# A message-passing layer on one core: the value product moved to the front of each step, the ranks to its end, and a bias written by ScalarE

## Chip, cores and metric

The kernel runs on one core of a Trainium2 chip. The metric is the device time of one execution in microseconds (us); the verdict rests on runs without a profile, and the traces come from one profiled execution of each kernel. The engines are TensorE (PE in the profile, PEld for its weight loads), VectorE (DVE), ScalarE (ACT), GpSimd (POOL) and SyncE (SP, which here only issues transfers).

## The reference

The program is one graph layer: 12,500 nodes with 128 features, 412,500 edges sorted by destination, 20 edge features.

```python
def ssp(x):
    return jax.nn.softplus(x) - LOG2
h = jnp.maximum(_layernorm(x), 0.0) @ W_in2f
Wij = (ssp(edge_attr_20 @ W_f1 + b_f1) @ W_f2 + b_f2) * edge_weight[:, None]
x_ij = h[dst] * Wij
agg = jax.ops.segment_sum(x_ij, src, num_segments=12500)
out = x + (ssp(agg @ W_o1 + b_o1) @ W_o2 + b_o2)
```

The gather goes by `dst`, which is sorted, and the sum by `src`, which is not. So each edge's message has to be carried to its source node's place.

## The kernel before

**Tiling.** The edges are cut into 806 chunks of 512 (`CH`), each of four tiles of 128 edges (`QT`). One pass of the main loop is one step: `step(k)` does one stage of work for each of some ten neighbouring chunks, so that each engine finds work. A chunk goes through these parts, each with a letter in the step's order:

- `Z` (L879): the hidden product, edge features by W_f1, into one of two PSUM banks `z`; done for chunk k+4. A sorted chunk (below) takes L875 instead.
- `L` (L885, L492, L493): ScalarE's three passes of softplus for chunk k+3, giving `a`.
- `E` (L892): VectorE joins `z` and `a` to `r` for chunk k+2; this also frees the bank `z`.
- the bias of the value (L1008 on TensorE, a product of ones with the bias; L1012 is the same write by ScalarE, `bias()` chooses by `"parts" in kept`). Letter `A` writes it for chunk k+1, letter `I` for chunk k+2.
- `V` (L1020): the value product, `r` by W_f2, onto the bias in a PSUM bank `v`; chunk k+1.
- `W` (L1000): VectorE builds the selection `at` for chunk k+3, and `P` (L1041): TensorE picks the 128 node rows of h for each edge with it, into another bank `v`; chunk k+2.
- `H` (L1057, L1064): ScalarE scales the picked rows by the edge weight to `hg`; chunk k+1.
- `M` (L1070): VectorE multiplies value and `hg` to the message `o` of chunk k. Then the chunk before it is scattered: four `DMA_INDIRECT` on GpSimd (L1086) write 129-float rows to HBM tables `slots`. `scatter()` makes the first of them wait for `sigs[-1]`, the last signal of TensorE that letter `U` kept (from chunk 24 on).
- `B` (L901), `R` (L950, L922), `T` (L930, L942, L945, L946): one-hot blocks, running ranks in the PSUM bank `counts`, and the reduction to the slot that each message goes to. They run up to six chunks ahead.
- `C` (L1172, L1166) and `S` (L1194): the sums. `slots` rows of finished segments are loaded back (`m`, L1152), VectorE compares them with place numbers (`to`), TensorE adds them up in `sums`; `K` (L1225) adds a block to the result.
- `X` (L1351 to L1404): TensorE's products of a presort of 80 chosen chunks (`SORT`), whose messages are later gathered and not scattered. `presorts()` is advanced once a step after chunk 14, and by `X` when its next piece is one of TensorE's. It ends by chunk 372 (`"idx" in kept`).
- `J`: small column work.

**What sets the order.** There is no scheduler: each engine does its instructions in the order in which the letters call them, and waits only for semaphores. Steps 0 to 7 take `FIRST_ORDER`, all others `ORDER`. Three banks `v` are handed round by the list `v_free`: pick, bias and value of neighbouring chunks take them, `H` and `M` give them back. The message tiles `o` are ten (`BACK`), and the second and third products of `V` and `P` wait for the scatters of ten chunks before (`behind`). Loads on SP wait for `sigs[-1]` as well (`covered`).

After the last chunk, the remaining sums and the output layer follow (some 170 us).

Of the kernel before, what the change touches and what calls it, by code (L numbers as in the profile page):

```python
# [60 lines left out]
def gnn_kernel(  # L61
# [33 lines left out]
    parts = next(n for n in range(3, SUMT + 1) if SUMT % n == 0)  # L95
# [47 lines left out]
    def sbuf(name, shape, dtype=F32):  # L143
        return const.tile(shape, dtype, name=name)
# [50 lines left out]
    idx = sbuf("idx", [P, NBLK], I32)  # L195
# [207 lines left out]
    kept = {}  # L403
# [224 lines left out]
    with tc.tile_pool(name="edge", bufs=2) as edge, tc.tile_pool(  # L628
# [860 lines left out]
        HEAD, SLOW, FREE, RA, RB = 8, 5, 12, 2, 6  # L1489
# [11 lines left out]
        def part(name, upto, make):  # L1501

            for j in range(made.get(name, -1) + 1, min(upto, NCH - 1) + 1):
                make(*of(j))
                made[name] = j
# [37 lines left out]
        def ahead(k):  # L1543
            return k + min(LR, RA + max(k, 0) // RB)

        ORDER, FIRST_ORDER = "TMHPRXEBCKSAVUZWJL", "MTBHVPWENISLJZRU"

        def step(k, units=(), order=None):

# [3 lines left out]
            def message(j):  # L1553
                if j in vs:
                    g, c = of(j)
                    g.message(c, vs[j], hgs.pop(j))
                    v_free.append(vs.pop(j))
                    waiting.append(j)
                    scatter()
# [95 lines left out]
            for c, u in due_gathers.get(k, ()):  # L1655
                c.gather(u)
            parts = {
                "E": lambda: part("end", min(k + EZ, made["log"]), hidden_end),
                "M": lambda: message(k),
                "N": lambda: message(k + 1),  # L1660
                "T": tops_of,
                "X": midway,
                "B": lambda: part("blocks", ahead(k + 1), blocks),
                "C": compares,
                "K": keep,
# [10 lines left out]
                "L": lambda: part("log", min(k + LL, made["hidden"]), hidden_log),  # L1676
                "U": signal,
            }
            for p in order or (FIRST_ORDER if k < HEAD else ORDER):
                parts[p]()  # L1680

        zeros = {}
# [35 lines left out]
        pos, k = 0.0, 0  # L1718
        jobs = {}
        for i, c in enumerate(collects[:-1]):  # L1720
            for u, (_, nb, _, nt) in enumerate(c.units):
                n = nb * nt
                for j in range(n):
                    pos = max(pos, at[i])
                    k = max(k, int(pos) + 1)
# [116 lines left out]
        with tc.manual_schedule():  # L1842
# [48 lines left out]
            hgs[0] = groups[0].picked(0, ps[0])  # L1891
            v_free.append(ps.pop(0))
            step(0, (), "M")
            part("log", 1, hidden_log)
            part("window", 1, window)
# [15 lines left out]
            part("blocks", 2, blocks)  # L1911
            part("window", 2, window)
            step(1, (), "M")
            next(moved, None)
            part("log", 2, hidden_log)
# [4 lines left out]
            for k in range(0, max(NCH, max(units) + 1)):  # L1920
                for seg, d in zeros.get(k, ()):
                    seg.clears.append(nc.sync.dma_start(*d).ins.name)
                now = units.get(k, ())
                for c, u in now:
                    if u == 0:
                        for i in range(AHEAD):
                            c.load(i)
                if k == NCH:
                    kept["rest"] = True
                step(k, now)  # L1930

                for _ in range(STAGES[k] if k < len(STAGES) else 1):
                    for m in h[:1]:
                        if next(m, 1) == 1:
                            h.pop(0)
                if k == 0:
                    early[1] = load_x(1)
                if k in ROWS:
                    kept["rows"] = ROWS[k]
                if k > NEXT - 3:  # L1940
                    next(aside, None)
                if k >= PRE and kept.get("want") != "mid":
                    kept["want"] = next(before_all, "mid")
                if k >= XK:
                    next(x_early, None)
# [136 lines left out]
```

## Time and profile before

| | us |
|---|---|
| median of three runs | 5035.33 (5027.56 to 5047.56) |
| the profiled execution's own time | 5080.24 |
| its span, first to last instruction | 5078.5 |
| steps 8 to 371 (with the presort), from the trace | 66.2 to 2024.3 |
| steps 372 to 805, from the trace | 2024.3 to 4910.9 |

No engine is busy for more than 77% of the span. In a row of the views, "idle before" is how long the engine stood still just ahead of those instructions, and the names behind the arrow are what ended it; "issue" and "remote" are waits whose end the profile cannot put to an instruction. The starts of TensorE's instructions are recorded, the ends of matmuls are modelled.

### The profile page before, as it was taken

The numbers are of one execution on the slowest core, as the hardware profiler recorded it, in microseconds if no ns is written. First come the engines' busy times: TensorE is split into PE (matmuls) and PEld (weight loads), VectorE is DVE, ScalarE is ACT, GpSimd is POOL, SyncE is SP. The second block draws the span as 40 slices with busy tenths as digits, with TensorE's granted clock in tenths as the row PEclk, the third lists the DMA queues.
The fourth block names the chain that finished last, engine by engine and source line by source line (L and its number), as shares of the span: only waits on it lengthen the run. The fifth ranks groups of instructions, "written<-read, shape, count | busy, mean of one in ns | idle before, by whom it ended". The sixth has DMA issues, their size and how long they took to land.

```text
span 5078.5 us, 78295 instructions
## 1 busy us (share of the span) xinstructions
PE 3908.5 (77%) x24114; PEld 2965.9 (58%) x24114; DVE 3200.6 (63%) x7639; ACT 2722.9 (54%) x6941; POOL 2957.1 (58%) x3100
## 2 busy tenths in 40 slices
PE   5667777777777777888888877778878887877879
PEld 3444545544444445666666665666666666666667
DVE  5767767666565667666655655565666666665657
ACT  6666666666666665555544444444444444444423
POOL 5555555555555556555666665666666665555543
PEclk8887878888777878999988988898999999898889
DMA  5566666665545655666655555655556655645547
GB/s 156 161 193 191 193 184 181 185 172 163 142 133 143 177 140 156 202 195 204 217 163 177 166 162 158 204 184 166 172 174 213 198 174 176 207 158 174 160 138 218
DMA packets 586009, 892.45 MB, mean 176 GB/s; under 512 B 164366, under 2 KB 368324, under 8 KB 585582
## 3 DMA queue, kind: packets, MB, share of 16 engines
q1 hardware_dynamic: 483584, 656.09, 43.8%
q0 software_dynamic: 100736, 230.77, 13.7%
q8 instruction: 192, 3.15, 0.3%
q14 instruction: 235, 1.93, 0.1%
q10 hardware_dynamic: 1262, 0.52, 0.0%
HBM read 490.45 MB, written 396.56 MB: 175 GB/s over the span
## 4 chain that ended last, share of the span: by engine, by line


## 5 line engine op out<-in xcount | busy, mean ns | idle before, releaser
L1086 POOL DMA_INDIRECT slots<-o,slot x2903 | 2806.1, 967 | 1819.1 <-issue 1287.3
L885 ACT ACTIVATE a<-z,bf 128x512 f32<-128x512 f32 x806 | 556.5, 690 | 1840.1 <-remote 838.1
L1194 PE MATMUL sums<-to,m 128*128 128x128 f32 x8296 | 1200.0, 299 | 181.1 <-issue 168.9
L1194 PEld LDWEIGHTS sums<-to,m 128*128 128x128 f32 x8296 | 1142.9, 213 | 267.5 <-issue 229.6
L1070 DVE TENSOR_TENSOR o<-v,hg 128x512 f32<-128x512 f32 x806 | 554.5, 688 | 1180.0 <-issue 566.0
L1020 PEld LDWEIGHTS v<-wf,r 128*128 128x128 f32 x6448 | 1002.7, 221 | 440.9 <-issue 383.1
L1020 PE MATMUL v<-wf,r 128*128 128x128 f32 x6448 | 1005.8, 305 | 49.4 <-issue 41.4
L1057 ACT ACTIVATE hg<-v,rcut 128x128 f32<-128x128 f32 x2904 | 818.9, 366 | 152.1 <-remote 83.5
L879 PE MATMUL z<-f,wf1z 128*128 128x512 f32 x1452 | 812.1, 641 | 40.2 <-DVE r L892 19.8
L1172 DVE TENSOR_TENSOR to<-counts,m 128x512 f32<-128x512 bf16 (+3 forms) x824 | 582.7, 740 | 347.9 <-remote 129.5
L1041 PEld LDWEIGHTS <-at 126*128 126x128 bf16 x2896 | 219.2, 103 | 722.1 <-issue 391.8
L892 DVE SCALAR_TENSOR_TENSOR r<-z,nbf,a 128x512 f32<-128x512 f32 x806 | 597.6, 741 | 1.7 <-ACT a L493 0.9
L493 ACT ACTIVATE a<-a,half 128x512 f32<-128x512 f32 x806 | 581.9, 722 | 26.2
L1008 PE MATMUL v<-hb 128*128 128x512 bf16 x784 | 339.8, 433 | 279.7 <-DVE o L1070 218.8
L930 DVE TENSOR_REDUCE top<-counts 128x4 f32<-128x392 f32 x726 | 403.9, 556 | 213.6 <-remote 148.9
L492 ACT ACTIVATE a<-a 128x512 f32<-128x512 f32 x806 | 507.9, 630 | 25.5
L1041 PE MATMUL v<-near,at 126*128 126x128 bf16 x2896 | 308.8, 232 | 257.4 <-DVE at L1000 133.3
L950 PE MATMUL counts<-inb,rest_of 128*128 128x392 f16 x719 | 258.8, 360 | 298.4 <-issue 149.2
L922 PEld LDWEIGHTS <-after 128*128 128x128 f16 x726 | 74.4, 102 | 339.0 <-issue 337.5
L879 PEld LDWEIGHTS z<-f,wf1z 128*128 128x128 f32 x1452 | 244.4, 210 | 47.3 <-issue 24.3
L922 PE MATMUL counts<-inb,after 128*128 128x392 f16 x726 | 264.0, 364 | 8.1 <-issue 7.8
L1000 DVE TENSOR_SCALAR at<-rel,prow 126x512 bf16<-126x512 bf16 x724 | 260.7, 360 | 0.0
(240 smaller groups left out, 2839.5 us busy)
## 6 DMA issues: line engine op xcount, KB each, us to landing
m<-slots SPq DMA_DIRECT2D x430, 258.0 KB
rel<-rel_d SPq DMA_DIRECT2D x201, 504.0 KB
m<-slots SPq DMA_DIRECT2D x178, 322.5 KB
m<-slots SPq DMA_DIRECT2D x139, 387.0 KB
f<-in_f_t SPq DMA_DIRECT2D x100, 512.0 KB
slots<-o,slot POOLq DMA_INDIRECT x2903
slots<-zero SPq DMA_DIRECT2D x88, 387.0 KB
slots<-zero SPq DMA_DIRECT2D x58, 516.0 KB
```

The lines of the kernel that those rows point to most:

```text
L492: nc.scalar.activation(a, a, AF.Exp, scale=-1.0)
L493: nc.scalar.activation(a, a, AF.Ln, bias=half, scale=0.5)
L879: kept["mm"] = nc.tensor.matmul(z_ps[k % 2], wf1z[:, k, :], self.f, start=True, stop=True)
L885: nc.scalar.activation(self.a[k], z_ps[k % 2], AF.Abs, bias=bf1)
L892: nc.vector.scalar_tensor_tensor(self.r[k], z_ps[k % 2], nbf1, self.a.pop(k), op0=ALU.max, op1=ALU.add)
L1020: mm = nc.tensor.matmul(v[:, i, :], r[:, i * P:(i + 1) * P], wf2, start=False, stop=True, skip_group_check=True)
L1041: mm = nc.tensor.matmul(ps[:, i, :], at[:, i * P:(i + 1) * P], near, start=i == 0, stop=i == QT - 1, skip_group_check=True)
L1057: act = nc.scalar.activation(hg[:, i, :], ps[:, i, :], AF.Copy, scale=cut[:, i:i + 1])
L1070: nc.vector.tensor_mul(self.o[c][:, :, :P], v, hg)
L1086: put = nc.gpsimd.indirect_dma_start(out=views[j % VIEWS], out_offset=bass.IndirectOffsetOnAxis(ap=self.slot[:, j:j + 1], axis=0), in_=o[: ...
L1172: nc.vector.tensor_tensor(to[:, :n, :], count_ps[:, None, :].to_broadcast([P, n, P]), m[:, :n, P:].to_broadcast([P, n, P]), op=ALU.is_equal)
L1194: kept["mm"] = nc.tensor.matmul(self.acc[b // QT][:, i, :], m[:, j, :P], to[:, j, :], start=t == 0, stop=t == self.tiles(b) - 1)
```

## The change

From step 8 on the letters stand in another order. Up to step 371 `ORDER` is `EMTBCKHAVXSPIWJZRLU`, from 372 on `LATE_ORDER`, the same without `X`. At step 372 the key `parts` is dropped, so that `bias()` writes with ScalarE (L1012) from there on. `I` now writes the bias two chunks ahead, so `A` finds it done. `U` is still the last letter, and the last product ahead of it is now one of `R` where `V` stood before.

```diff
-        ORDER, FIRST_ORDER = "TMHPRXEBCKSAVUZWJL", "MTBHVPWENISLJZRU"
+        ORDER, FIRST_ORDER = "TMHPRXEBCKSAVUZWJL", "MTBHVPWENISLJZRU"
+        LATE_ORDER, LATER = "EMTBCKHAVSPIWJZRLU", 372
+        ORDER = "EMTBCKHAVXSPIWJZRLU"
...
-            for p in order or (FIRST_ORDER if k < HEAD else ORDER):
+            if k == LATER:
+                assert "idx" in kept
+                del kept["parts"]
+            for p in order or (FIRST_ORDER if k < HEAD else ORDER if k < LATER else LATE_ORDER):
                 parts[p]()
```

By engine, a step's letters read before and after: TensorE `P R X S A V Z` and `V X S P I Z R`; VectorE `T M E B C K W J` and `E M T B C K W J`; ScalarE `H L` and `H L`, from 372 on `H I L`.

TensorE in the second stage, before. `v` with its number is one of the three banks, `hb_76` holds the bias parts; the first row is the last product of a pick:

```order
L1041 MATMUL v_161<-near,at 128x128
L950 LDWEIGHTS rest_of
L950 MATMUL counts<-inb,rest_of 128x392
L922 LDWEIGHTS after
L922 MATMUL counts<-inb,after 128x392
L1194 MATMUL sums_157<-to,m 128x128 x8
L1008 LDWEIGHTS hb_76
L1008 MATMUL v_160<-hb_76 128x512
L1020 MATMUL v_160<-wf_63,r 128x128 x4
L879 MATMUL z_155<-f,wf1z 128x512
```

The same stretch of work after, from the hidden product of one step to the pick of the next:

```order
L879 MATMUL z_155<-f,wf1z 128x512
L950 LDWEIGHTS rest_of
L950 MATMUL counts<-inb,rest_of 128x392
L922 LDWEIGHTS after
L922 MATMUL counts<-inb,after 128x392
L1020 MATMUL v_159<-wf_63,r 128x128 x4
L1194 MATMUL sums_158<-to,m 128x128 x8
L1041 LDWEIGHTS at
L1041 MATMUL v_159<-near,at 128x128
```

The bias product is gone from TensorE, the value product stands ahead of the sums, the pick behind them, and the ranks behind the hidden product. Before, every value product goes to bank `v_160`; after, the banks take turns, and a value product's bank comes back in the pick behind the sums.

VectorE in the second stage, before: one step, from `at` to `at`.

```order
L1000 TENSOR_SCALAR at<-rel,prow 126x512
L930 TENSOR_REDUCE top<-counts 128x4
L1070 TENSOR_TENSOR o<-v_160,hg 128x4x128
L892 SCALAR_TENSOR_TENSOR r<-z_156,nbf_67,a 128x512
L901 TENSOR_TENSOR inb<-of_block,blk_30709 128x392
L1172 TENSOR_TENSOR to<-counts,m 128x512
L1000 TENSOR_SCALAR at<-rel,prow 126x512
```

And after:

```order
L1000 TENSOR_SCALAR at<-rel,prow 126x512
L892 SCALAR_TENSOR_TENSOR r<-z_156,nbf_67,a 128x512
L1070 TENSOR_TENSOR o<-v_160,hg 128x4x128
L930 TENSOR_REDUCE top<-counts 128x4
L901 TENSOR_TENSOR inb<-of_block,blk_30707 128x392
L1172 TENSOR_TENSOR to<-counts,m 128x512
L1000 TENSOR_SCALAR at<-rel,prow 126x512
```

`r` has moved ahead of the message, and the reduction `top` behind it.

ScalarE in the second stage, before:

```order
L1057 ACTIVATE hg<-v_161,rcut 128x128 x4
L1064 ACTIVATE o<-place 128x4
L885 ACTIVATE a<-z_155,bf_66 128x512
L492 ACTIVATE a<-a 128x512
L493 ACTIVATE a<-a,half 128x512
```

And after:

```order
L1057 ACTIVATE hg<-v_160,rcut 128x128 x4
L1064 ACTIVATE o<-place 128x4
L1012 ACTIVATE v_160<-bf_84 128x512
L885 ACTIVATE a<-z_156,bf_66 128x512
L492 ACTIVATE a<-a 128x512
L493 ACTIVATE a<-a,half 128x512
```

The bias write stands between the scaling and the softplus, into the bank that the scaling has just read.

## The prediction

> **What bounds the kernel now.** I read the page's busy line first, then the two stages (with the presort, and after it), then TensorE's waits in each, then the timeline of one period, and last the rows of the engines that the change loads or unloads.
>
> ```profile
> span 5078.5 us, 78295 instructions
> PE 3908.5 (77%) x24114; PEld 2965.9 (58%) x24114; DVE 3200.6 (63%) x7639; ACT 2722.9 (54%) x6941; POOL 2957.1 (58%) x3100
> ```
>
> No engine is full: the time lies in round trips between engines. By stretch (columns: us, busy time of PE, PEld, DVE, ACT and POOL with counts, granted clock, DMA share, GB/s):
>
> ```profile
> 66.20:2024.30 1958.10, 1407.74 (x7896) 949.95 (x7896) 1296.29 (x3638) 1251.18 (x3290) 1129.01 (x1162) 0.81 0.58 167
> 2024.30:4910.90 2886.60, 2320.85 (x14999) 1866.28 (x14999) 1748.10 (x3674) 1380.40 (x3481) 1736.50 (x1802) 0.91 0.57 180
> ```
>
> The first stage is 364 steps of 5.38 us, the second 434 of 6.65. TensorE is idle for some 550 us in each (1958.1 - 1407.7, 2886.6 - 2320.9). What it waited for, by instruction group, two rows of the first stage and then three of the second (busy, mean ns of one | idle before, what ended it):
>
> ```profile
> L1008 PE MATMUL v<-hb 128*128 128x512 bf16 x351 | 159.8, 455 | 239.9 <-DVE o L1070 191.8 <-issue 29.0 <-DVE top L918 12.8
> L950 PE MATMUL counts<-inb,rest_of 128*128 128x392 f16 x293 | 109.5, 374 | 258.8 <-issue 130.0 <-DVE top L930 119.1 <-DVE pre L1400 6.0
> ...
> L1194 PE MATMUL sums<-to,m 128*128 128x128 f32 x7666 | 1115.3, 299 | 169.3 <-issue 164.8 <-DMA near<-h 1.6
> L1008 PE MATMUL v<-hb 128*128 128x512 bf16 x434 | 180.4, 416 | 39.9 <-DVE o L1070 26.9 <-issue 10.5 <-DVE top L918 2.0
> L1041 PE MATMUL v<-near,at 126*128 126x128 bf16 x1704 | 180.2, 229 | 250.8 <-DVE at L1000 133.3 <-issue 80.3 <-DVE to L1172 12.5
> ```
>
> In the first stage TensorE waits ahead of the bias product for VectorE's message, which gives the bank back, and ahead of the ranks for the reduction `top`. In the second it waits mostly ahead of the pick for `at`. One period of the second stage (start, duration, engine, what, idle before it):
>
> ```profile
> 2403.55 1.05 PE L1020 MATMUL v<-wf,r 128*128 128x128 f32 x8
> 2404.44 1.02 PE L879 MATMUL z<-f,wf1z 128*128 128x512 f32 x2
> ...
> 2405.30 0.39 PE L1041 MATMUL v<-near,at 126*128 126x128 bf16 x4
> ...
> 2405.52 0.33 PE L950 MATMUL counts<-inb,rest_of 128*128 128x392 f16 x1
> ...
> 2405.69 0.33 PE L922 MATMUL counts<-inb,after 128*128 128x392 f16 x1
> ...
> 2406.11 0.96 POOL L1086 DMA_INDIRECT slots<-o,slot  x1 [0.30 <-issue]
> ...
> 2408.98 0.69 ACT L885 ACTIVATE a<-z,bf 128x512 f32<-128x512 f32 x1 [4.56 <-remote]
> 2408.99 0.69 DVE L1070 TENSOR_TENSOR o<-v,hg 128x512 f32<-128x512 f32 x1 [4.41 <-issue]
> ...
> 2409.65 0.95 POOL L1086 DMA_INDIRECT slots<-o,slot  x1 [2.58 <-issue]
> ...
> 2418.53 0.96 POOL L1086 DMA_INDIRECT slots<-o,slot  x1 [0.31 <-issue]
> ...
> 2421.27 0.69 DVE L1070 TENSOR_TENSOR o<-v,hg 128x512 f32<-128x512 f32 x1 [1.70 <-remote]
> ...
> 2421.93 0.96 POOL L1086 DMA_INDIRECT slots<-o,slot  x1 [2.44 <-issue]
> ```
>
> This is the picture to keep. The value product ends at 2404.6 and the hidden product at 2405.5, yet the message and the softplus that need nothing else start only at 2408.98, both at once: TensorE's signals reach the others up to 4.4 us late. They come after GpSimd has run dry (its last scatter ends at 2407.07). Then the message runs, GpSimd gets its next scatters, and after eight of them, two chunks, it is dry again: 2409.65 to 2421.93 is 12.28 us for two steps, of which 8 x 1.26 = 10.1 is scattering and 2.4 to 2.6 the gap. So in the second stage two things set the pace together: round trips that carry a late signal, and GpSimd's two chunks to a period. GpSimd's scatters, the first stage and the second:
>
> ```profile
> L1086 POOL DMA_INDIRECT slots<-o,slot x1162 | 1130.2, 973 | 830.1 <-issue 476.4 <-PE v L1020 96.7 <-ACT o L1064 70.2
> ...
> L1086 POOL DMA_INDIRECT slots<-o,slot x1707 | 1643.1, 963 | 963.0 <-issue 794.4 <-ACT a L885 57.6 <-DVE inb L901 21.9
> ```
>
> Back to back, one takes 0.97 + 0.30 = 1.27 us: 1476 us of the first stage's 1958, 2156 of the second's 2887.
>
> **The change, part by part.** I sum against the profiled execution's 5080.24 us; the median of the runs is 5035.33, a factor of 0.9912, and the sum is scaled by it at the end.
>
> (a) *First stage, the bias and value products.* Before, the value product ends a step, the message waits for its signal, and the next bias product waits for the message. After, the bias goes two chunks ahead into the bank that ScalarE's scaling has freed, and the value product needs only that and `r`. The message's bank is now needed by the pick, behind the next value product, the presort's products and the sums. The signal's slack grows by at least one value product (1.05 us) and mostly by a half step or more. The wait of 239.9 us has 351 products behind it; a typical one:
>
> ```profile
> 861.06 0.69 DVE L1070 TENSOR_TENSOR o<-v,hg 128x512 f32<-128x512 f32 x1 [5.45 <-issue]
> ...
> 861.80 0.58 PE L1008 MATMUL v<-hb 128*128 128x512 bf16 x1 [4.79 <-DVE o L1070]
> ```
>
> Bounds: all of it goes (-240), or all comes back ahead of the ranks or the pick (0). The ranks' loop is not loosened: before, ranks to `top` to ranks; after, ranks to `top`, blocks, compare, ranks, since the compare reads the same PSUM bank that the ranks write. That loop still passes one late signal a step, and its row (258.8 us) is as large as the one that goes. I take half: **-120 us**.
>
> (b) *Second stage, the pick.* Before, `at` stands on VectorE behind a compare that waits for the ranks of the same step, so the pick of the next step waits for a late signal of the ranks. After, the compare follows the ranks of the step before, and `at` of a pick is built a whole step ahead. So the 250.8 us can go; bounds -251 and 0. But here each period also holds GpSimd's two chunks and its gap, which the order of TensorE does not shorten; TensorE's gain turns into waiting unless a third chunk's signal slips into the period. I take a quarter, nearest to that bound: **-60 us**.
>
> (c) *Second stage, the bias on ScalarE.* TensorE loses 434 products. Their issue distance, from a bias product to the value product behind it, is small:
>
> ```profile
> 2414.41 0.38 PE L1008 MATMUL v<-hb 128*128 128x512 bf16 x1
> 2414.41 1.08 PEld L1020 LDWEIGHTS v<-wf,r 128*128 128x128 f32 x8
> 2414.62 1.05 PE L1020 MATMUL v<-wf,r 128*128 128x128 f32 x8
> ```
>
> 434 x 0.21 = 91 us, and the wait ahead of them was 39.9: at most -131. ScalarE gets as many writes; the first steps show what one takes, and the second row is where ScalarE stands idle in the second stage:
>
> ```profile
> L1012 ACT ACTIVATE v<-bf x22: 580/601/602, 13.5 to 142.1; 128x512 f32<-128x512 f32 x22
> ...
> L885 ACT ACTIVATE a<-z,bf 128x512 f32<-128x512 f32 x431 | 296.8, 689 | 1355.7 <-remote 588.6 <-PE z L879 332.5 <-PE counts L922 206.7
> ```
>
> 434 x 0.601 = 261 us, just ahead of a softplus that waits 1355.7 / 431 = 3.1 us each time. Behind the write is queued that softplus, then `r`, then (new) the message, which now stands behind `r` on VectorE. While the 3.1 us of cover last, the write costs nothing; without them it would be up to +261. I take **0** for both ends together.
>
> (d) *The signal that releases scatters and loads.* It was the value product's, it is now the ranks'. Both are the last of their step but one product, and between two of them lies one step of TensorE's work in either order. From release to the next signal TensorE needed, before, the message (0.69), bias and value products (0.21 + 1.05); after, the message, `top`, blocks and compares, then the ranks:
>
> ```profile
> L1172 DVE TENSOR_TENSOR to<-counts,m 128x512 f32<-128x512 bf16 (+3 forms) x731 | 522.4, 750 | 317.9 <-remote 129.5 <-PE z L879 67.9 <-PE v L1020 48.4
> L1070 DVE TENSOR_TENSOR o<-v,hg 128x512 f32<-128x512 f32 x432 | 297.3, 688 | 757.7 <-issue 416.0 <-remote 198.7 <-PE v L1020 42.3
> L930 DVE TENSOR_REDUCE top<-counts 128x4 f32<-128x392 f32 x423 | 234.9, 555 | 11.4 <-remote 4.9 <-PE z L879 4.3 <-issue 2.0
> L901 DVE TENSOR_TENSOR inb<-of_block,blk 128x392 f16<-128x392 bf16 x421 | 148.7, 353 | 0.0
> ```
>
> That is 0.69 + 0.56 + 0.35 + 1.7 compares x 0.75 + ranks 0.5 = 3.4 us against 2.0. GpSimd has 4 x 1.26 = 5.0 us of work in that time, so I take **0**; the other end is the rival below. A signal that comes sooner could not run GpSimd faster than it does: no gain here.
>
> (e) Everything else moves without a price: `r` ahead of the message waits for a softplus of the step before, covered by the 757.7 us for which VectorE stands idle ahead of the message; the presort's products stand behind the value product (1.05) where they stood behind pick and ranks (0.39 + 0.5), so ScalarE's and VectorE's half of a presort piece has the same time; SP's loads wait for the same signal as the scatters.
>
> Sum: -120 - 60 + 0 + 0 = -180; 5080 - 180 = 4900, times 0.9912 = **4860 us**.
>
> TensorE's products keep program order, says the Trainium skill (TensorE: Matmul & The Clock Gate, "Step-by-step: what each phase is for"): only weight loads are pulled ahead. By that alone a wait that goes would be met again at the next instruction that needs the same signal, (a) would be 0 and the sum 5080 - 60 = 5020, scaled 4976 us. The rows of the first stage are on its side in part: bias product and ranks wait in turn, 239.9 and 258.8.
>
> **The rivals.**
> 1. *No change.* GpSimd's period of two chunks holds, and in the first stage the ranks' wait swallows what the bias product's gave. For it: 12.28 us a period whatever TensorE does in between. Against it: the first stage's GpSimd is dry for 1958 - 1476 = 482 us, so there it is not the bound. Time: 5035, give or take 25. Chance 0.17.
> 2. *Slower: the ranks' signal comes too late for the second chunk of a period.* It decides from 5.0 us after the release: 3.4 us worked out in (d) plus a lateness of 1.6. Signals in the middle of a period were late by more (4.4 above). Each time GpSimd then runs dry after one chunk and pays a gap of 2.5 us more. The second stage has 1707 / 4 = 427 scattered chunks, 213 periods; a third of them gives +178, all +530. The same in the first stage would add to it. Time: about 5210, from 5080 to 5560. Chance 0.23.
> 3. *More: the clock goes up too.* The granted clock is 0.81 in the first stage, where TensorE idles for 28% of it, and 0.91 in the second, where it idles for 20%. If the first stage got the second's clock, its 1407.7 us of busy time would shrink by 1 - 0.81/0.91 = 11%, 155 us, on top: about 4710. Chance 0.10. The Trainium skill's clock gate (TensorE: Matmul & The Clock Gate, Part 1) bears on it: an idle window of about 3.4 us halves the clock, a busy one restores it; the gaps of 4 to 5 us above are of that length, and the new order would have to close them whole.
>
> **How the numbers follow.** My forecast has 0.50. With rival 3, faster has 0.60; rival 1 is same, 0.17; rival 2 slower, 0.23. About 0.5% is what a measurement of this kernel can tell from no change. The range: below, (a) and (b) both at three quarters give -370, scaled 4670, and I go to 4660; rival 3's lower part lies outside. Above, it takes in rival 1 and the mild half of rival 2, to 5130. Outside remain some 0.07 below and 0.13 above. If it is faster, 4700 to 4990 is the likely part.
>
> **What the trace after would show.** (a) right: no wait for the message ahead of a bias product, and the ranks' idle in the first stage not above some 380 us; wrong: L950 or L1041 idles there by 500. (b) right: L1041's wait for `at` below 100 us. (c) right: L1012 at 0.6 us, 434 more, ScalarE's idle ahead of L885 smaller by as much. (d) right: still eight scatters between GpSimd's long gaps in the second stage; wrong: four. What would make the forecast wrong is (d) above all, since late signals are not explained by anything that this trace shows, and I assume that they stay as late as they are.

## The result, and the profile after

The changed kernel takes 5097.89 us (median of 4 runs, 5091.94 to 5109.76) beside 5034.40 for the kernel before: a ratio of 1.012, with a 95% interval of 1.0102 to 1.0138. It is slower by 63 us, where I had forecast 4860 and faster. The runs below were made in five sets: in three, as in all numbers so far, the kernel before takes about 5040 us and TensorE's signals come late, in the other two it takes 3992 us and they come promptly, and each run is compared with the kernel before of its own set.

The page of the changed kernel, its span and busy line:

```profile
span 5097.5 us, 76863 instructions
PE 3795.7 (74%) x23681; PEld 2890.9 (57%) x23681; DVE 3202.9 (63%) x7639; ACT 2952.9 (58%) x7374; POOL 2963.4 (58%) x3100
```

The stages, with the columns as in the prediction (us, busy time of PE, PEld, DVE, ACT, POOL, granted clock, DMA share, GB/s), from the value product of chunk 8 to those of chunks 372 and 805. First the changed kernel, then a second profile of the kernel before, which I took because the first one (5080 us) was 45 us above the median:

```profile
68.90:2079.10 2010.20, 1361.21 (x7873) 924.04 (x7872) 1286.29 (x3630) 1253.32 (x3286) 1128.10 (x1159) 0.82 0.56 162
2079.10:4926.80 2847.70, 2253.90 (x14588) 1815.93 (x14586) 1762.17 (x3685) 1606.93 (x3912) 1740.96 (x1802) 0.90 0.58 183
```

```profile
59.70:2010.80 1951.10, 1401.54 (x7897) 950.15 (x7897) 1296.24 (x3638) 1252.73 (x3291) 1130.32 (x1163) 0.81 0.58 168
2010.80:4856.70 2845.90, 2310.85 (x15000) 1843.66 (x14999) 1748.37 (x3676) 1378.62 (x3480) 1735.95 (x1801) 0.91 0.58 183
```

So the loss lies in the first stage: 2010.2 against 1951.1, +59 us (+52 against the first profile). The second stage is unchanged: 2847.7 against 2845.9. The 2886.6 us of the first profile, on which my sum stood, were a long execution. The granted clock hardly moved (0.82 and 0.90 against 0.81 and 0.91).

What TensorE waited for in the first stage, after (busy, mean ns of one | idle before, what ended it):

```profile
L1008 PE MATMUL v<-hb 128*128 128x512 bf16 x350 | 152.6, 436 | 71.6 <-issue 47.2 <-ACT hg L1057 24.0
L1041 PE MATMUL v<-near,at 126*128 126x128 bf16 x1164 | 127.1, 239 | 180.2 <-DVE o L1070 98.9 <-issue 67.7 <-DVE r L892 13.4
L950 PE MATMUL counts<-inb,rest_of 128*128 128x392 f16 x293 | 113.2, 386 | 96.5 <-DVE top L930 53.5 <-issue 39.4 <-DVE to L1172 3.6
L1351 PE MATMUL sums<-pick,pre 107*128 107x2 bf16 x320 | 21.2, 170 | 188.7 <-ACT pre L1407 124.5 <-issue 62.5 <-ACT hb L454 1.7
L1373 PE MATMUL sums<-ones,pre 128*98 128x1 f16 x320 | 35.3, 214 | 75.4 <-DVE pre L1344 68.8 <-issue 4.2 <-DVE pre_d L1333 2.4
```

In the second profile of before the same rows read:

```profile
L1008 PE MATMUL v<-hb 128*128 128x512 bf16 x351 | 160.7, 458 | 285.7 <-DVE o L1070 237.7 <-issue 31.0 <-DVE top L918 9.8
L950 PE MATMUL counts<-inb,rest_of 128*128 128x392 f16 x293 | 109.1, 372 | 220.7 <-issue 107.3 <-DVE top L930 106.9 <-DVE pre L1400 4.7
L1041 PE MATMUL v<-near,at 126*128 126x128 bf16 x1164 | 124.6, 234 | 3.1 <-issue 1.5 <-DVE at L1000 1.4 <-DVE early_room L266 0.2
L1373 PE MATMUL sums<-ones,pre 128*98 128x1 f16 x320 | 31.8, 203 | 0.0
L1351 PE MATMUL sums<-pick,pre 107*128 107x2 bf16 x320 | 21.3, 170 | 9.8 <-ACT pre L1407 4.9 <-issue 4.8
```

The wait for the message ahead of the bias product is gone, and the ranks' wait fell from 220.7 us to 96.5. Part of the message's wait is met again at the pick, L1041, which now stands idle for 180.2 us, 98.9 of them for the message, where it had 3.1. And two rows that were hardly there have grown: products of the presort, L1351 and L1373, now wait 264 us where they had waited 10.

In the second stage, after:

```profile
L1041 PE MATMUL v<-near,at 126*128 126x128 bf16 x1704 | 186.6, 230 | 65.3 <-issue 42.6 <-DVE o L1070 10.2 <-DMA slots<-o,slot 5.8
L950 PE MATMUL counts<-inb,rest_of 128*128 128x392 f16 x418 | 148.4, 355 | 236.4 <-DVE to L1172 133.3 <-issue 69.2 <-DVE to L1166 31.9
```

The pick's wait for `at` (133.3 us in the first profile, 97.3 in the second) is gone, and the ranks wait for the compare instead (133.3 and 31.9 us): no less waiting, one instruction further on. That the figure 133.3 stands twice is chance.

GpSimd's scatters in the first stage, of the second profile of before and of the changed kernel:

```profile
L1086 POOL DMA_INDIRECT slots<-o,slot x1163 | 1131.7, 973 | 821.1 <-issue 468.8 <-PE v L1020 123.3 <-ACT o L1064 63.0
```

```profile
L1086 POOL DMA_INDIRECT slots<-o,slot x1159 | 1129.4, 974 | 883.1 <-issue 331.8 <-ACT a L885 174.4 <-ACT a L492 133.7
```

GpSimd's idle time grew by 62 us, as the stage did. Where it grew can be read from the scatters' single rows in the trace: a presorted chunk has no scatter, so GpSimd always runs dry there. From chunk 25 to 371 the 73 gaps behind such chunks add up to 281 us in the second profile of before and 391 after, all other gaps of over 0.5 us to 218 and 156. Of the 73, before, 14 are over 5 us; after, 40, most of them 7 to 8. One of these, from the timeline of the changed kernel (start, duration, engine, line, what, idle before it):

```profile
860.09 1.03 PE L1404 MATMUL sums<-pre,pre_d 128*107 128x512 bf16 x4
...
867.75 0.96 POOL L1086 DMA_INDIRECT slots<-o,slot  x1 [0.30 <-issue]
868.98 0.60 ACT L1407 ACTIVATE pre<-sums 107x512 bf16<-107x512 f32 x1 [4.37 <-remote]
...
869.63 0.25 PE L1351 MATMUL sums<-pick,pre 107*128 107x2 bf16 x4 [2.98 <-issue]
870.47 0.57 DVE L1344 TENSOR_TENSOR pre<-counts,pre 128x392 f16<-128x392 bf16 x1 [5.43 <-remote]
...
871.09 0.49 PE L1373 MATMUL sums<-ones,pre 128*98 128x1 f16 x4 [1.21 <-DVE pre L1344]
...
875.18 0.53 PE L922 MATMUL counts<-inb,after 128*128 128x392 f16 x1
...
876.47 0.96 POOL L1086 DMA_INDIRECT slots<-o,slot  x1 [7.76 <-ACT a L885]
```

The presort's product ends at 861.1, but ScalarE's copy of it starts only at 868.98, 0.3 us after GpSimd's last scatter: the late signal. ScalarE had been idle for 4.37 us by then. TensorE, which has issued its next value product, stands at L1351 for that copy. Only then can it do the pick, the hidden product and the ranks, and GpSimd's next scatter waits for the ranks' signal; it starts 0.76 us after their end. In 39 of the 40 long gaps TensorE's longest stop is at L1351 or L1373, and the scatter starts 0.75 us (median) after the ranks.

### The profile page after: what moved, and what is told of

Same layout as the page of the kernel before. It is cut to its first block, busy times and chain, and to the rows that moved or that the text cites. A ratio compares the mean times of both kernels' runs of the same rounds, so it can differ in the third digit from the quotient of the medians.

```text
span 5097.5 us, 76863 instructions
## 1 busy us (share of the span) xinstructions
PE 3795.7 (74%) x23681; PEld 2890.9 (57%) x23681; DVE 3202.9 (63%) x7639; ACT 2952.9 (58%) x7374; POOL 2963.4 (58%) x3100
## 4 chain that ended last, share of the span: by engine, by line
## 5 line engine op out<-in xcount | busy, mean ns | idle before, releaser
L1194 PEld LDWEIGHTS sums<-to,m 128*128 128x128 f32 x8296 | 1097.8, 208 | 272.9 <-issue 264.1
L1020 PEld LDWEIGHTS v<-wf,r 128*128 128x128 f32 x6448 | 953.9, 214 | 179.3 <-issue 134.8
L1020 PE MATMUL v<-wf,r 128*128 128x128 f32 x6448 | 980.5, 298 | 68.0 <-issue 63.4
L879 PE MATMUL z<-f,wf1z 128*128 128x512 f32 x1452 | 881.0, 691 | 33.9 <-issue 18.5
L1041 PE MATMUL v<-near,at 126*128 126x128 bf16 x2896 | 316.7, 234 | 245.5 <-issue 110.2
L1041 PEld LDWEIGHTS <-at 126*128 126x128 bf16 x2896 | 245.3, 105 | 318.7 <-issue 249.8
L879 PEld LDWEIGHTS z<-f,wf1z 128*128 128x128 f32 x1452 | 277.0, 216 | 82.0 <-issue 53.4
L1012 ACT ACTIVATE v<-bf 128x512 f32<-128x512 f32 x455 | 273.7, 602 | 0.0
```

The lines of the kernel that those rows point to most:

```text
L879: kept["mm"] = nc.tensor.matmul(z_ps[k % 2], wf1z[:, k, :], self.f, start=True, stop=True)
L1020: mm = nc.tensor.matmul(v[:, i, :], r[:, i * P:(i + 1) * P], wf2, start=False, stop=True, skip_group_check=True)
L1041: mm = nc.tensor.matmul(ps[:, i, :], at[:, i * P:(i + 1) * P], near, start=i == 0, stop=i == QT - 1, skip_group_check=True)
L1194: kept["mm"] = nc.tensor.matmul(self.acc[b // QT][:, i, :], m[:, j, :P], to[:, j, :], start=t == 0, stop=t == self.tiles(b) - 1)
```

## The experiments

The stage times are those of each run's own profile. The last column counts the gaps of over 5 us behind presorted chunks. The ratio is to the kernel before in the same set.

| kernel (sets with late signals) | median us | ratio, interval | stage 1 | stage 2 | long gaps |
|---|---|---|---|---|---|
| before, second profile | 5026 (one run) | | 1951 | 2846 | 14 |
| after, again | 5076.87 | 1.007, 1.0032 to 1.0107 | 2022 | 2851 | 43 |
| bias_on_tensor_2 | 5087.52 | 1.0097, 1.007 to 1.0124 | 2020 | 2839 | 41 |
| new_second_only_2 | 5042.03 | 0.9985, 0.996 to 1.001 | 1957 | 2846 | 19 |
| signal_behind_value_2 | 4998.19 | 0.9904, 0.9882 to 0.9926 | 1884 | 2877 | 9 |
| first_stage_signal | 4965.02 | 0.9857, 0.9829 to 0.9884 | 1893 | 2836 | 12 |
| message_first | 4965.78 | 0.9848, 0.9811 to 0.9885 | 1884 | 2843 | 8 |
| presort_behind_ranks | 5028.36 | 0.9984, 0.9959 to 1.0009 | 1948 | 2842 | 8 |
| presort_last_signal_early | 5032.29 | 0.9992, 0.9971 to 1.0013 | 1951 | 2843 | 5 |
| message_first_presort_last | 5045.43 | 1.0013, 0.9992 to 1.0034 | 1960 | 2844 | 12 |
| signal_ahead_of_value | 5185.90 | 1.0297, 1.0269 to 1.0325 | 2099 | 2840 | 53 |
| scatters_ahead_loads_behind | 5175.27 | 1.0266, 1.0231 to 1.0302 | 2091 | 2833 | 54 |

| kernel (sets with prompt signals) | median us | ratio, interval | stage 1 | stage 2 |
|---|---|---|---|---|
| new_first_only | 3992.43 | 1.0005, 0.9996 to 1.0014 | 1490 | 2287 |
| new_second_only | 3986.72 | 0.9986, 0.9977 to 0.9996 | 1484 | 2274 |
| signal_behind_value | 3982.11 | 0.9976, 0.9968 to 0.9985 | 1483 | 2269 |
| bias_on_tensor | 3986.39 | 0.9991, 0.9982 to 1.0001 | 1484 | 2270 |
| signal_behind_pick | 3989.00 | 0.9990, 0.9980 to 0.9999 | 1488 | 2273 |
| presort_ahead_of_value | 3989.05 | 0.9991, 0.9981 to 1.0000 | 1487 | 2286 |

**First set: which stage, which part.** The edits, each against the changed kernel:

```diff
 new_first_only:      - LATE_ORDER = "EMTBCKHAVSPIWJZRLU", del kept["parts"]
                      + LATE_ORDER = "TMHPRXEBCKSAVUZWJL", parts kept
 new_second_only:     - ORDER = "EMTBCKHAVXSPIWJZRLU"   + ORDER = "TMHPRXEBCKSAVUZWJL"
 signal_behind_value: + ORDER = "EMTBCKHAVUXSPIWJZRL", LATE_ORDER = "EMTBCKHAVUSPIWJZRL"
 bias_on_tensor:      - del kept["parts"]
```

new_first_only: 

> New order for chunks 8 to 371 alone; from 372 on the order of before, bias on TensorE. Theory A (the loss is in the first stage: after a presorted chunk, whose step has no scatter, GpSimd waits for the ranks at the end of a whole TensorE step, 7 to 9 us instead of 2.5 to 5): slower than before by the first stage's 52 us or more, 5085 to 5140 us. Theory B (the loss is in the second stage, by the bias on ScalarE or the late ranks, and a long profiled run of before hides it): within 25 us of before, 5010 to 5060.

new_second_only: 

> The order of before up to chunk 371; from 372 on the new order with the bias on ScalarE. Theory A: the second stage gains some 40 us, 4980 to 5020 us. Theory B: slower than before by all of the change's loss, 5080 to 5110.

signal_behind_value: 

> The changed kernel, but scatters and loads wait for the value product again (its signal is taken behind V) and not for the ranks. Theory A: the 40 gaps of over 5 us behind presorted chunks shrink from some 7.6 to 4.5 us, about -120 us: 4950 to 5010 us, and no more than 15 such gaps. Rival C (the presort's products behind the value product bring their signals late to ScalarE and VectorE, whatever the scatters wait for): the gaps stay, 5080 to 5115.

bias_on_tensor: 

> The changed kernel with the bias still written by TensorE from chunk 372 on; the order stays. This prices term (c) of the prediction, which was 0 between -131 and +261 us. Theory A: the second stage's time is set by the late signals and GpSimd, and the writer of the bias does not matter: 5098 give or take 25. Theory B: ScalarE's 434 writes of 0.60 us delay the softplus, and the kernel is faster without them by 60 us or more, below 5040.

In these four the signals came promptly, and all lie within 0.24% of before (table). That is a result of its own: without late signals neither half of the change moves the time by more than 0.14%. The whole change was not run there. The order of before in its first stage there (in new_second_only), by stretch and by GpSimd:

```profile
55.80:1539.50 1483.70, 1208.69 (x7898) 831.83 (x7897) 1293.36 (x3639) 1235.90 (x3290) 1115.93 (x1145) 0.94 0.76 220
```

```profile
L1086 POOL DMA_INDIRECT slots<-o,slot x1145 | 1117.3, 976 | 368.1 <-issue 236.1 <-ACT o L1064 13.6 <-DMA slots<-o,slot 11.6
```

1484 us is close to the 1476 us that the scatters take back to back. The 73 gaps behind presorted chunks add up to 39 us here, against 281 with late signals, so there was no loss to explain, and the theories, whose times all rest on late signals, were not told apart.

**Second set, with late signals.** The changed kernel, the kernel before, and two of the edits above once more.

after_again: 

> The changed kernel again. The runs so far fall into two kinds: executions of 5034 to 5098 us, in which TensorE's signals reach the others several us late, and the four of the stage experiments at 3982 to 3992 us, with no such signal. If signals arrive promptly here too, theory A expects no loss, since no gap behind a presorted chunk exists to grow: 3975 to 3995 us beside 3992 for before. If they are late, it expects the loss again: 1.0 to 1.4% above before.

before_again: 

> The kernel before again, for a second profile. With prompt signals: near 3992 us, first stage about 1490 us (GpSimd's 1476 with hardly a gap). With late signals: near 5035 us, and the stage that is shorter than in the profiled run of 5080 us tells where the rest of the change's loss lies.

signal_behind_value_2: 

> The changed kernel, with scatters and loads waiting for the value product. With late signals, theory A: 4950 to 5010 us and no more than 15 gaps over 5 us behind presorted chunks in the first stage; rival C (the presort's products behind the value product are what comes late): 5080 to 5115 and some 40 gaps. With prompt signals: within 0.5% of before, as in its first run (3982).

new_second_only_2: 

> New order and ScalarE's bias from chunk 372 on alone. With late signals, theory A: the second stage gains some 40 us of 5034, so 4980 to 5020; theory B (the loss is in the second stage): 5080 to 5110. With prompt signals: within 0.5% of before, as in its first run (3987).

The loss is there again, and again in the first stage (2022), but with 0.7% it is smaller than the 1.0 to 1.4% expected. The profiled execution of after_again is the longest of its four (5111 against a median of 5077), so its 2022 is at the upper end. The new order from 372 on alone costs and gains nothing (5042, stage 2846): theory B is out, and A's gain of 40 us in the second stage too, since the 2887 it rested on was chance. Taking the signal behind the value product again cuts the long gaps from 43 to 9 and the first stage by 138 us, to 1884; theory A had said 120 for the whole. Its second stage came out some 30 us longer, which led to the next run.

**Third set: the signal's place, the presort's place, the bias.**

```diff
 first_stage_signal:    + ORDER = "EMTBCKHAVUXSPIWJZRL"  (LATE_ORDER as in the change)
 presort_behind_ranks:  + ORDER = "EMTBCKHAVSPIWJZRXLU"
 signal_ahead_of_value: + ORDER = "EMTBCKHAUVXSPIWJZRL"
 bias_on_tensor_2:      - del kept["parts"]
```

first_stage_signal: 

> The changed kernel, with the scatters' and loads' signal taken behind the value product for chunks 8 to 371 alone; from 372 on it is the ranks' as in the change. With late signals, theory A: first stage about 1885 us as with the value's signal throughout (2010 to 2022 changed, 1951 to 1958 before), second stage about 2849 as in the changed kernel, against 2877 with the value's signal throughout; so 4950 to 4990 us, 1.5% below before. If those 27 us of the second stage were chance, 4990 to 5010. With prompt signals: 3975 to 3995.

presort_behind_ranks: 

> The changed kernel, with the presort's products moved from behind the value product to behind the ranks; the scatters' signal stays that of the ranks, at the end. With late signals, theory A: the long gaps behind presorted chunks stay, some 1 us shorter, since the ranks come sooner by the presort's products: 5040 to 5100 us, over 30 gaps. Rival C (the presort's late signals to ScalarE and VectorE, 490 us of idle in the first stage): the gaps go, 4980 to 5020 us. With prompt signals: 3975 to 3995.

signal_ahead_of_value: 

> As first_stage_signal, but the signal is taken ahead of the value product: it is the ranks' of the step before, a whole step earlier than in the change. With late signals, theory A: the earlier the signal, the shorter the gap behind a presorted chunk (sum over the first stage 391 to 409 us with the ranks' signal, 199 with the value's): 100 to 199 here, and the first stage 1790 to 1885 us; total 4880 to 4990. If the gap is by then set by the message and the late signals themselves, the same as first_stage_signal. With prompt signals: 3970 to 3995.

bias_on_tensor_2: 

> The changed kernel with the bias still written by TensorE from chunk 372 on, again. With late signals this prices term (c), which I put at 0 between -131 and +261 us: 0 means the changed kernel's 5077 to 5098 us, second stage 2848 to 2851 us; theory B (ScalarE's writes delay the softplus) means 5040 or less. With prompt signals: 3980 to 3995, as before.

The first came out as said, 4965 us: 1.4% below before and 2.2 to 2.6% below the change; with message_first below it is the fastest with late signals. Its two stages:

```profile
63.80:1956.80 1893.00, 1358.43 (x7871) 921.71 (x7870) 1291.92 (x3628) 1248.02 (x3281) 1134.97 (x1163) 0.85 0.60 173
1956.80:4793.20 2836.40, 2256.02 (x14588) 1820.46 (x14587) 1763.71 (x3686) 1608.00 (x3918) 1736.68 (x1799) 0.90 0.58 183
```

A gap behind a presorted chunk in its timeline, to be laid beside the one above:

```profile
1112.68 0.96 POOL L1086 DMA_INDIRECT slots<-o,slot  x1 [0.31 <-issue]
...
1115.94 0.25 PE L1351 MATMUL sums<-pick,pre 107*128 107x2 bf16 x4 [1.85 <-ACT pre L1407]
1116.59 0.68 DVE L1070 TENSOR_TENSOR o<-v,hg 128x512 f32<-128x512 f32 x1
...
1118.12 0.96 POOL L1086 DMA_INDIRECT slots<-o,slot  x1 [4.47 <-DVE top L942]
...
1120.16 0.48 PE L922 MATMUL counts<-inb,after 128*128 128x392 f16 x1
```

TensorE stands at L1351 here too, but the scatter does not wait for what comes behind that stop: it starts 0.85 us after the message and 2 us ahead of the ranks. With the ranks' signal, by my estimate, it would have started 0.75 us behind their end, at about 1121.4, and the gap would be 7.7 us, which is the size of those of the change. The stops have shrunk as well: L1351 and L1373 wait 44 us in this stage, against 264 in the change. So the stop is no fixed price that the signal either meets or avoids; with the ranks' signal it is six times as long.

The second run fitted neither theory. With the presort behind the ranks and the signal still theirs, the long gaps are gone (8) and so is the loss, but the first stage is 1948 and not 1890: A had said that they stay, C that 4980 to 5020 would come out. The third refuted the simple reading of A, that an earlier signal is always better: with the signal just ahead of the value product (the ranks' of the step before) the first stage takes 2099 us. Its rows, TensorE's pick in the first stage and one long gap:

```profile
L1041 PE MATMUL v<-near,at 126*128 126x128 bf16 x1164 | 132.8, 246 | 444.9 <-DVE o L1070 314.5 <-issue 110.2 <-DVE r L892 19.6
```

```profile
1224.61 0.96 POOL L1086 DMA_INDIRECT slots<-o,slot  x1 [0.30 <-issue]
...
1231.06 0.68 DVE L1070 TENSOR_TENSOR o<-v,hg 128x512 f32<-128x512 f32 x1
...
1232.59 0.96 POOL L1086 DMA_INDIRECT slots<-o,slot  x1 [7.03 <-DVE top L942]
```

The gap now ends with the message (0.85 us behind it, in the median of 53), and TensorE waits for the message too. The scatters run further ahead: in the first stage 61 rows of exactly twelve scatters, three chunks, run without a gap of over 1.5 us, against 25 in first_stage_signal. TensorE's late signals come mostly while no scatter runs (the numbers are in the last section). So I read a longer row as a longer silence, with the whole round to the next message in one gap. This is a reading and not shown: the changed kernel, too, has 43 such rows of twelve (the second profile of before 15), and a pick that waits about as long (498.6 us) stands in a stage of 1951 us below. The fourth run prices the bias: 5087.5 without ScalarE's writes, second stage 2839 against 2848 and 2851. Nothing that can be told from zero.

**Fourth set: do signal and presort act through one stop?**

```diff
 presort_last_signal_early:   + ORDER = "EMTBCKHAVUSPIWJZRXL"
 message_first:               + ORDER = "MTEBCKHAVUXSPIWJZRL"
 message_first_presort_last:  + ORDER = "MTEBCKHAVUSPIWJZRXL"
 scatters_ahead_loads_behind: + ORDER = "EMTBCKHAYVUXSPIWJZRL"; Y keeps a second signal, which
                                scatter() waits for; loads wait for U's
```

presort_last_signal_early: 

> As first_stage_signal (signal behind the value product up to chunk 371), with the presort's products behind the ranks besides. Theory D (what costs is that TensorE stops at the presort's first product, for a late signal, while the ranks and so the scatters' signal are still to come; either move takes the signal out of that stop's way): the presort's place no longer matters, first stage 1870 to 1910 us, total 4945 to 4985. Theory C2 (the presort's place has a price of its own, the 68 us between 2016 and 1948): first stage about 1820, total about 4900. With prompt signals: 3970 to 3995.

message_first: 

> As first_stage_signal, with the message ahead of r on VectorE up to chunk 371. After a stop the message stands behind r, which waits for 2.0 us of softplus. If the remaining gaps behind presorted chunks (203 us together) hang on that, they fall to some 120 and the first stage from 1893 to about 1810: 4880 us. If not, 4950 to 4985; above 4990 if r then comes late to the value product. With prompt signals: 3970 to 3995.

message_first_presort_last: 

> Both moves of the two runs beside it together. If neither has an effect of its own: 4945 to 4985 us. If the effects add, as theory C2 and the message's wait would have it: about 4810.

scatters_ahead_loads_behind: 

> As signal_ahead_of_value, but only the scatters take the signal ahead of the value product; the loads of SyncE keep the one behind it. That kernel lost 206 us in the first stage against first_stage_signal. If the scatters' early release does it (three chunks are scattered in a row, TensorE's signals are held back for all 15 us of it, and one gap of 7 to 9 us follows): first stage 2080 to 2110 us, total 5170 to 5190. If the loads' early start does it: first stage about 1893, total about 4965.

Half of theory D stands: with the presort behind the ranks the signal's place no longer matters (1951 against 1948), while with it behind the value product it is worth 117 to 138 us. The other half fell: the two do not end at the same 1890 but at 1950. The message's place on VectorE does nothing (1884 against 1893), and added to the presort's move it does nothing either (1960, total 5045, where 4945 to 4985 or 4810 had been expected): the remaining gaps do not hang on it. The last run shows that the early release of the scatters, not that of the loads, costs the 200 us (2091). In the other direction, from the value product to the ranks, no run moves the two apart.

presort_last_signal_early says something more. In the first stage it differs from before by the new order alone: the presort stands behind the ranks and the signal behind the value product, as they did. Its first stage takes 1951 us, as before, and the pick now has the wait:

```profile
L1041 PE MATMUL v<-near,at 126*128 126x128 bf16 x1164 | 127.5, 240 | 498.6 <-DVE o L1070 327.7 <-issue 108.0 <-DVE r L892 60.7
```

**Fifth set: the stop or the distance?**

```diff
 signal_behind_pick:     + ORDER = "EMTBCKHAVXSPUIWJZRL"
 presort_ahead_of_value: + ORDER = "EMTBCKHAXVUSPIWJZRL"
```

signal_behind_pick: 

> As first_stage_signal, but the signal is the pick's: in the same place as the value's, except that the presort's products (and with them TensorE's stop for a late signal) now stand ahead of it; the ranks still come behind it. Theory E (the loss needs a stop of TensorE ahead of the signal that feeds GpSimd): first stage 1990 to 2020 us as with the ranks' signal, total 5065 to 5095. Theory F (only the distance counts, from the value product to the ranks some 4 us): first stage 1900 to 1930, total 4975 to 5005. With prompt signals: 3970 to 3995.

presort_ahead_of_value: 

> As first_stage_signal, but the presort's products stand ahead of the value product, whose signal still feeds scatters and loads. Theory E: the stop stands ahead of the signal again, and the first stage is like the changed kernel's, 1990 to 2022 us, total 5065 to 5095. Theory F: the signal comes later by the presort's products alone (about 1.5 us in two steps of three), first stage 1890 to 1930, total 4965 to 5005. With prompt signals: 3970 to 3995.

In both the signals came promptly (3989, as before), where E and F say the same. So these two runs do not tell them apart. For E stand the two timelines above and where TensorE stands in 39 of 40 long gaps. Against F as the whole account speaks the pair of 1948 and 1951: with the presort out of the way, the sums, the pick, the bias, the hidden product and the ranks still lie between the signal's two places, and yet the place is worth nothing. What holds that pair at 1950 is not known, so this is no proof.

## Why the prediction was wrong

The first stage by the two moves that I priced apart, all in the new order with late signals (us; before takes 1951 to 1958):

| | signal behind the value product | signal behind the ranks |
|---|---|---|
| presort behind the ranks | 1951 | 1948 |
| presort behind the value product | 1884 to 1893 | 2010 to 2022 (the change) |

- **(a) The first stage's order: 0, not -120.** With presort and signal left where they were, the new order brings nothing (1951): the wait for the message is met again at the pick, which was the other bound of my range. The first stage gets shorter by 58 to 74 us (1884 to 1893) only when the presort's products move behind the value product as well. The test that I named in the trace (no wait for the message ahead of the bias product, ranks not above 380 us) came out right while the stage grew. The test looked at three of TensorE's rows, and the larger part of the new waiting stood in two others.
- **(d) The release signal: this is the step that failed.** I put 0 for moving it from the value product to the ranks. With the presort's products between the two places, as in the change, it measured +117 to +138 us in the first stage, and that turns some -65 into +59. With the presort behind the ranks it measured nothing (1948 against 1951). My sum counted the engines' own work up to the ranks (3.4 us) against a chunk's 5.0 us of scattering. It missed two things: that behind a presorted chunk there is no scattering to hide anything, and that TensorE may stop for a late signal between the signal's old and new place. That the stop does it, and not the mere distance, rests on the traces. In the second stage, which has 7 presorted chunks and none of the presort's products, (d) was right, and the signal behind the value product even came out longer there (2877 against 2833 to 2851, one profile).
- **(e) The presort's move is not free.** I called it so because the half steps of ScalarE and VectorE stayed as long. It is worth -58 to -67 us with the signal behind the value product and +62 to +74 with the signal behind the ranks, where TensorE's waits ahead of L1351 and L1373 went from 10 to 264 us. (d) and (e) were each priced alone; the loss is in the two together.
- **(b) The pick's wait: 0, not -60.** It went, as the test asked (no wait for `at`), and came back ahead of the ranks: the two rows together wait 302 us after, and 290 and 238 in the two profiles of before. Against (a) I had set that TensorE's products keep program order (the Trainium skill, TensorE: Matmul & The Clock Gate, "Step-by-step: what each phase is for"). What I drew from it holds here and in (a): a wait that goes is met again at the next product that needs the same round trip. GpSimd's rhythm held, as rival 1 had it for this stage: between gaps of over 2 us stand 153 rows of eight scatters (156 in the second profile of before) and 29 of four (30). My picture of two chunks to a period came from one period, though; with gaps of over 1.5 us counted, 98 rows of four stand beside 145 of eight.
- **(c) The bias on ScalarE: 0, as said.** ScalarE has 432 writes more, and its idle time has mostly changed place:

```profile
L1057 ACT ACTIVATE hg<-v,rcut 128x128 f32<-128x128 f32 x1700 | 482.8, 366 | 1164.6 <-remote 702.9 <-PE v L1041 198.6 <-PE v L1020 108.5
L885 ACT ACTIVATE a<-z,bf 128x512 f32<-128x512 f32 x432 | 289.9, 671 | 6.7 <-remote 3.1 <-PE counts L922 2.0 <-PE v L1041 1.0
L1012 ACT ACTIVATE v<-bf 128x512 f32<-128x512 f32 x432 | 259.9, 602 | 0.0
```

Before, the first of these rows read:

```profile
L1057 ACT ACTIVATE hg<-v,rcut 128x128 f32<-128x128 f32 x1704 | 478.9, 362 | 86.1 <-remote 35.1 <-PE v L1020 16.2 <-issue 11.8
```

The idle ahead of the softplus fell from 1355.7 to 6.7 us and that ahead of the scaling rose from 86.1 to 1164.6: 270 less together, and the writes take 260. 434 products less on TensorE moved nothing either.
- **The rivals.** Rival 2 (the ranks' signal too late, then GpSimd dry) was the one that came, with its price at the lower end, but not where I put it: it was to show in the second stage as four scatters between gaps, and it came in the first, behind presorted chunks. Rival 3 did not come. That the time lies within my range all the same is luck: the range went so far up for a second stage that got slower, and it did not.

## What to carry to other kernels

Before moving a signal that another engine waits for, list every instruction between its old and its new place and ask of each what it waits for: a stop there can be added to the receiver's wait (7.8 us in the one gap above, 4.5 in the other). If a change moves such an instruction and the signal at once, price the two together. Price the wait at the place where the receiver has nothing queued (here the step without a scatter), not at its average load. And profile the kernel before twice before building on a stage's time: the 41 us by which one stage varied were two thirds of the effect.

## What the runs showed of the hardware

- **The late signals are TensorE's alone.** The traces hold the updates of the semaphores themselves. In the second profile of before, 1420 of TensorE's 2868 recorded updates come more than 0.3 us after the last signalling product that ended before them, and 1064 more than 1 us. Of VectorE's 3375 only 6 come so late and of ScalarE's 2462 only 2; with prompt signals (new_second_only) it is 2 of TensorE's 3500. Of the 1420 late ones, 1202 (85%) come while no scatter runs on GpSimd, and of VectorE's updates 40% do. What links the two is not shown. With late signals, about half of VectorE's and ScalarE's updates have no record in the trace.
- **Late signals belong to a set of runs, not to the kernel.** In the sets with prompt signals, kernels of the same kind take 3982 to 3992 us, before among them. The chips on record are numbers 2, 5 and 8 for the late sets and 0 and 8 for the prompt ones. Number 8 stands on both sides, so it is not shown that the lateness is a property of one chip. The transfers are no faster with prompt signals: queue q1's packets fill 43.8% of 5078 us in before and 57.0% of 3985 in new_second_only, 2224 and 2271 us of engine time. What is missing there are the waits that the profile puts to "issue" and "remote". In the second stage of before, VectorE's idle ahead of the message was 757.7 us, 614.7 of it such waits; the same order with prompt signals (new_first_only):

```profile
L1070 DVE TENSOR_TENSOR o<-v,hg 128x512 f32<-128x512 f32 x434 | 298.2, 687 | 272.7 <-ACT o L1064 73.6 <-DMA slots<-o,slot 71.1 <-PE v L1020 40.5
```

  The granted clock goes with it, 0.95 to 0.97 against 0.86 to 0.89; which follows from which is not shown, and why TensorE's signals are late was not found. The Trainium skill (Perfetto Trace Analysis, "Tensor Engine Instruction (MATMUL, LD_WEIGHTS)") says that a matmul's signal follows PSUM's acknowledgement and that its end in the profile is an estimate. In the changed kernel's stretch above, the time from that end to the start of the instruction that waits for it goes from 0.1 us (the hidden product's end at 862.42, its softplus at 862.50) to 7.9 us (L1404 to L1407).
- **The receiver's pace has a best place.** With the presort behind the value product, the first stage took 2099 us with the signal just ahead of it, 1884 to 1893 with it behind the value product (three profiles), and 2010 to 2022 with it behind the ranks (three profiles). As I read the traces, too late holds GpSimd behind TensorE's stops, and too early lets it run ahead and then stand still for one whole round. Every order with the presort behind the ranks, that of before included, took 1948 to 1960 us, whatever the signal; why stays open.
